# A graph layer in three-word float32 products: two samples as plain float32 products from raw weights, token rows moved to products 7 and 15, loads and buffers planned anew

## The chip, the cores and the metric

The kernel runs on one core of one Trainium2 chip. The metric is the device time of one execution in microseconds. The parts of the core have short names here, those of the profile: PE is TensorE (PEld its weight loads), DVE is VectorE, ACT is ScalarE, POOL is GpSimd, and SP is the queue from which nearly all DMAs are issued.

## The reference

There are 64 samples of 256 tokens with 768 features, and a 256x256 matrix of links for each. The links are 0 or 1 in the inputs of this case.

```python
h = relu(layernorm(x))                        # each [256, 768]
ctx = (adj @ (h @ Wadj.T + badj)) / max(deg, 1)
ctx += (adj.T @ (h @ Wrev.T + brev)) / max(rdeg, 1)
ctx += h @ Wself.T + bself
rel = agg @ Wr.T + br * deg                   # agg: sums over the links of E[rel]
rel += ragg @ Wrr.T + brr * rdeg
out = x + ctx + rel
```

With links of 0 and 1, everything in `rel` and all biases depend only on the two degrees of a token, so they come down to a product of a few "token rows" (degree and whether it is over zero) with a few rows made once from E, Wr, Wrr and the biases. What is left is three products of h with 768x768 weights, and two products with the links, called aggregates.

## The kernel before

**Fast products with 15 instead of 18.** A sample's h has two halves of 128 tokens (`a` and `b`), each cut in three along the features (`a0 a1 a2 b0 b1 b2`). The three weights are cut in three along the same dimension; block "21" is third 2 of weight 1 (0 is Wadj, 1 Wself, 2 Wrev). Together they are a matrix product of 2x3 by 3x3 blocks. The table `PRODUCTS` does it with 15 block products: each has a left side that is a sum of h blocks, and a right side that is a sum of weight blocks. Each block product is added to one or two of six results, `c00 c01 c02 c10 c11 c12` (token half, weight).

**Words.** [...]both sides are split in words: a left in three (`left0, left1, left2`), a right in three (`word0, word1, word2`), and a block product is three word products (L523, in `passes`). Each word product is 4 matmuls of 128x384 (two feature blocks, two halves of the outputs). Between them ACT multiplies the accumulator by a scale factor (`scale`, L559), and at the end ACT or DVE moves or adds it to its result (`read`, L568, L577, L579). Left words are made by ACT and DVE from h and from sums of h that POOL makes (L485 to L512). Right words are made once for each product in `prepare`: DVE sums raw weight blocks (`right`, L434), ACT and DVE take the words (L446 to L460). Products in `ON_PE` (11 and 3) have their sums and words formed on PE by plain float32 products with the identity (L397, L402), in a PSUM bank pair called `hold`.

**Two sweeps.** The words of 15 products don't fit beside the rest, so all 64 samples go through products 5, 10, 8, 11, 14, 3, 13 and 2 first, then all of them through 9, 7, 6, 15, 12, 4 and 1. Between the sweeps h and five of the results are stored to DRAM (`keep`) and loaded again. In sweep 1 `front1` loads x and its transpose, takes mean and variance on DVE (`bn_stats`, L598), turns them into a row on PE (the turn, L609), sends this through DRAM to all partitions (`d`, `row`), and POOL and DVE make h from them (centre L628, norm L632). In sweep 2 `front2` loads h, results and links, and makes token rows from the degrees; `step2` ends with high and low words of four results (`hl`, L762 and L766), the aggregates (L778, L789) and the store of the output. The token rows are added in `product` as two matmuls (L547) each in products 4 (rows of the half `a`, with weight -1, read into both c01 and c11), 12 (all, -1) and 1 (all, +1).

**A planner sets the order.** `record` notes each step with its engine, a duration in us, a rank (the time at which it is wanted, moved by a table `OFFSETS` of one number for each kind of step), and what it reads and writes. `Plan.schedule` then plays the engines: each takes the step of lowest rank that is ready, and the order that comes out is the order of the program. Each engine runs its steps in that order. Steps marked `lock` keep DVE and POOL out of each other's way. Buffers come in classes, handed out in order of rank, a slot being free once the last step on its buffer has ended: 

```python
SLOTS = {"W": 24, "B": 17, "T": 5, "A": 3, "S": 8, "Q": 4, "U": 2}
```

W holds two thirds-of-a-weight rows (6 KB a partition): raw blocks, words, hl pairs. B holds one row of 768 or a left's words: x, h, lefts, results, right sums. A holds links and rows, S small things, T sums of h, Q pairs of PSUM banks (one of them is `hold` in sweep 1), U the two halves of `hold`: turns, and copies of left0 that DVE subtracts from (`top`). The 8 products of sweep 1 have 24 words, as many as W has slots.

Of the kernel before, what the change touches and what calls it, by code (L numbers as in the profile page):

```python
# [14 lines left out]
ALU = mybir.AluOpType  # L15
# [39 lines left out]
    (  # L55
        (5, "y", 0, ((1, 1, 0),)),
        (10, "z", 0, ((1, 1, 2),)),
# [5 lines left out]
        (2, "z", 1, ((1, 0, 1),)),  # L63
# [3 lines left out]
        (7, "v", 0, ((1, 0, 1), (1, 0, 2))),  # L67
        (6, "x", 1, ((1, 0, 1),)),
        (15, "u", 0, ((1, 1, 1), (1, 1, 2))),
# [7 lines left out]
SLOTS = {"W": 24, "B": 17, "T": 5, "A": 3, "S": 8, "Q": 4, "U": 2}  # L77
ON_PE = (11, 3)
APART = ("22", "20", "00", "21", "01")
AHEAD = 5.0  # L80
OVERLAP = {"DVE": 0.08, "ACT": 0.095, "POOL": 0.045, "PE": 0.17}
PERIOD = (17.2, 21.4)
PREPARE = (6.0, 4.5)
LEAD = 5.0
OFFSETS = {
    "a0+a1+b0+b1": 6.92, "a0+a1+b0+b1@": 10.33, "a0+a2": -4.36, "a0+a2+b0+b2": -15.26, "a0+a2+b0+b2@": -101.36,
    "a0+a2+b2": -43.25, "a0+a2+b2@": 18.8, "a0+a2@": -65.24, "a1+a2": -1.7, "a1+a2@": -90.48, "a1+b0+b1": -2.76,
    "a1+b0+b1@": 37.03, "a1+b1": -4.89, "a1+b1@": 8.33, "a2+b2": -62.32, "a2+b2@": 0.73, "adj": 7.74,
    "adj@": 11.96, "agg00": -22.66, "agg00@": -1.8, "agg01": 14.01, "agg01@": -4.15, "agg10": 18.9,
    "agg10@": -19.08, "agg11": 18.57, "agg11@": -53.92, "aggr": -58.89, "aggr@": 7.86, "b0+b1": -35.52,  # L90
    "b0+b1@": 20.73, "b1+b2": -58.71, "b1+b2@": 9.34, "b2-a1": -78.11, "b2-a1@": 23.55, "bias": -93.82, "c00": 4.1,
    "c00@": -32.32, "c01": -13.38, "c01@": -25.73, "c02": -10.98, "c02@": -58.58, "c10": 15.35, "c10@": -16.49,
    "c11": 4.28, "c11@": 28.03, "c12": 5.06, "c12@": 22.74, "centre0": -2.99, "centre0@": 48.24, "centre1": -36.36,
    "centre1@": -19.74, "cols": 59.3, "d": 8.44, "d@": -26.79, "degree": 4.86, "degree@": -25.5,
    "diagonal": -16.03, "eT": -2.45, "eps": -58.84, "eps@": -14.98, "first 1": -13.18, "first 10": -32.05,
    "first 10@": 36.33, "first 11": -73.71, "first 11@": 12.34, "first 12": -23.58, "first 12@": 24.72,
    "first 13": 13, "first 13@": 11.63, "first 14": -45.99, "first 14@": -0.54, "first 15": -64.88,
    "first 15@": -7.01, "first 1@": -53.22, "first 2": -17.08, "first 2@": -7.79, "first 3": -22.76,
    "first 3@": 0.32, "first 4": -5.82, "first 4@": -10.53, "first 5": 2.67, "first 5@": -21.18, "first 6": 9.55,
    "first 6@": 9.11, "first 7": -39.56, "first 7@": -22.92, "first 8": 23.14, "first 8@": -81.1,  # L100
    "first 9": -31.59, "first 9@": 29.93, "flag": 58.21, "h0": -17.13, "h0@": -14.79, "h1": 5.1, "h1@": -12.91,
    "half": -17.88, "half@": 39.87, "high00": 15.93, "high00@": 11.46, "high02": 33.87, "high02@": -65.71,
    "high10": 25.4, "high10@": -16.28, "high12": 14.73, "high12@": 16.2, "keep c00": -2.76, "keep c00@": -66.74,
    "keep c01": -49.17, "keep c01@": -17.21, "keep c02": -13.78, "keep c02@": 16.72, "keep c10": 2.56,
    "keep c10@": 27.78, "keep c12": -24.16, "keep c12@": 54.25, "keep h0": 57.82, "keep h0@": -13.43,
    "keep h1": 50.58, "keep h1@": -14.32, "left0 1": -19.12, "left0 10": -0.78, "left0 10@": 2.36, "left0 11": 5.7,
    "left0 11@": -57, "left0 12": 8.66, "left0 12@": 24.55, "left0 13": -10.65, "left0 13@": -53.6,
    "left0 14": -7.4, "left0 14@": 10.04, "left0 15": 0.45, "left0 15@": 13.09, "left0 1@": 20.01,
    "left0 2": -12.83, "left0 2@": -17.63, "left0 3": -44.32, "left0 3@": -29.15, "left0 4": -4.81,
    "left0 4@": -12.38, "left0 5": -15.48, "left0 5@": -6.26, "left0 6": 2.81, "left0 6@": 24.35,  # L110
    "left0 7": -43.92, "left0 7@": 8.32, "left0 8": -31.57, "left0 8@": -6.64, "left0 9": -73.51,
    "left0 9@": -13.5, "left1 1": -49.91, "left1 10": -0.8, "left1 10@": 36.7, "left1 11": 0.1,
    "left1 11@": -17.36, "left1 12": -16.79, "left1 12@": 17.57, "left1 13": -27.91, "left1 13@": 14.45,
    "left1 14": 25.3, "left1 14@": -1.57, "left1 15": 15.44, "left1 15@": -42.21, "left1 1@": -89.54,
    "left1 2": -4.18, "left1 2@": -18.11, "left1 3": 12.77, "left1 3@": -67.25, "left1 4": 21.43,
    "left1 4@": -23.96, "left1 5": -21.51, "left1 5@": 43.61, "left1 6": -76.57, "left1 6@": -33.58,
    "left1 7": 12.56, "left1 7@": 3.34, "left1 8": -17.95, "left1 8@": -11.83, "left1 9": -33.48,
    "left1 9@": -40.82, "left2 1": 15.98, "left2 10": -45.72, "left2 10@": -5.31, "left2 11": 13.71,
    "left2 11@": 13.79, "left2 12": 17.14, "left2 12@": -36.12, "left2 13": -80, "left2 13@": -73.73,
    "left2 14": 27.23, "left2 14@": 27.84, "left2 15": 5.95, "left2 15@": -6.41, "left2 1@": -31.13,  # L120
    "left2 2": 15.55, "left2 2@": -37.29, "left2 3": -26.89, "left2 3@": 75.78, "left2 4": 28.79,
    "left2 4@": 23.04, "left2 5": -17.53, "left2 5@": -19.13, "left2 6": 4.2, "left2 6@": 31.92, "left2 7": -35.03,
    "left2 7@": 20.55, "left2 8": -3.06, "left2 8@": 34.27, "left2 9": 2.47, "left2 9@": -7.4, "less of": -8.17,
    "line": -16.84, "line@": -70.49, "load raw00": -11.53, "load raw01": -9.83, "load raw02": -2.61,
    "load raw10": -14.49, "load raw11": 0.43, "load raw12": -8.47, "load raw20": -2.81, "load raw21": -1.61,
    "load raw22": -10.89, "low00": -25.5, "low00@": 22.91, "low02": 6.14, "low02@": 45.31, "low10": -11.25,
    "low10@": -20.56, "low12": 27.22, "low12@": -26.51, "minus": -23.89, "minus@": -6.49, "norm0": 12.4,
    "norm0@": 48.54, "norm1": 5.92, "norm1@": 4.71, "out0": -45.84, "out0@": 42.05, "out1": 4.37, "out1@": 69.47,
    "pick": -1.48, "plus": -23.43, "plus@": -44.43, "pow": -36.89, "pow@": -93.72, "rd": -32.96, "rd@": -55.47,
    "read 1": -39.73, "read 10": -30.69, "read 10@": 2.04, "read 11": -26.47, "read 11@": 28.3, "read 12": 6.94,  # L130
    "read 12@": 27.17, "read 13": 3.76, "read 13@": 6.54, "read 14": 16.39, "read 14@": 26.9, "read 15": 25.66,
# [37 lines left out]
def kind_of(name):  # L169
    kind, _, last = name.rpartition(" ")  # L170
    if not last.isdigit():
        return name
    return kind + "@" if last == "0" and not kind.endswith(" of") else kind
# [915 lines left out]
```

## Time and profile before

| | us |
|---|---|
| median of 3 runs | 2620.19 (2619.38 to 2621.8) |
| the profiled execution | 2618.8 |
| its span | 2617.0 |
| PE busy | 2526.7 (97%) |
| PE weight loads busy | 2446.6 (93%) |
| DVE busy | 2209.1 (84%) |
| ACT busy | 1877.9 (72%) |
| POOL busy | 1312.8 (50%) |
| DMA, mean | 228 GB/s |

The span is what the profiler records, from the first instruction to the last; the execution's own time is 1.8 us more. Busy times of PE are modelled and overlap from one matmul to the next, so that a long row of matmuls always reads as fully busy; how fast PE advances is better read from the starts of its instructions in the timeline. The table of busy time by stretch, the chain of waits (followed back from the end, at each step to what released it) and the timeline are views of the same trace. A name such as "L523 PE MATMUL y<-word,left" is a line of the kernel, an engine, and output and inputs by the program's names.

### The profile page before, as it was taken

The page shows a single profiled execution, that of the slowest core. Times are in us where ns is not written, and L with a number is a line of the kernel's source. Part 1 is how long each engine was busy: PE and PEld are TensorE (multiplying, and loading weights), DVE is VectorE, ACT ScalarE, POOL GpSimd, SP SyncE. Part 2 cuts the span into 40 slices and gives each one's busy share as a digit, 9 for nine tenths or more (in the row PEclk, how much of TensorE's full clock was granted, in tenths as well). Part 3 has the DMA queues.
Part 4 walks back from the last instruction along what each step waited for, and adds up shares of the span by engine and source line. Part 5 has one row for each costly group of instructions (what it writes and reads, how often), then busy time and mean ns, then how long its engine had stood idle before and what let it go on. Part 6 is the DMA issues. An engine that isn't in the chain of part 4 may idle for free.

```text
span 2617.0 us, 44548 instructions
## 1 busy us (share of the span) xinstructions
PE 2526.7 (97%) x14154; PEld 2446.6 (93%) x14154; DVE 2209.1 (84%) x4007; ACT 1877.9 (72%) x4045; POOL 1312.8 (50%) x1160
## 2 busy tenths in 40 slices
PE   5999999999999999997999999999999999999998
PEld 2899999999999999986899999999999999999998
DVE  6877777777777777777999999999999999999997
ACT  4888888888888888887666666666666666666664
POOL 2454554445445445442555555555555555555554
PEclk8999999999999999998999999999999999999999
DMA  5677777777777777776566656555666666666563
GB/s 195 223 258 258 265 255 269 264 261 259 258 261 254 259 263 258 259 252 221 177 219 207 210 206 212 206 206 206 211 215 212 212 213 215 216 207 210 206 211 130
DMA packets 225815, 595.39 MB, mean 228 GB/s; under 512 B 24340, under 2 KB 24596, under 8 KB 225576
## 3 DMA queue, kind: packets, MB, share of 16 engines
q1 hardware_dynamic: 225576, 592.51, 65.1%
q8 instruction: 112, 1.84, 0.3%
q14 instruction: 127, 1.04, 0.1%
HBM read 365.79 MB, written 226.62 MB: 226 GB/s over the span
## 4 chain that ended last, share of the span: by engine, by line
PE 79%; DVE 6%; DMA 4%; ACT 4%; POOL 4%; issue 3%; SPq 0%; POOLq 0%; DVEq 0%; ACTq 0%
PE x L523 20%; PE y L523 13%; PE agg L778 13%; PE z L523 7%; PE w L523 6%; PE u L523 5%; PE v L523 5%; PE t L523 5%; DMA h<-in_x_t_dram 3%; POOL h L628 2%; PE x L547 2%; ACT hold L502 1%; ACT left L495 1%; DVE stats L598 1%; PE t L547 1%
## 5 line engine op out<-in xcount | busy, mean ns | idle before, releaser
L766 POOL TENSOR_TENSOR hl<-c,hl 128x768 fp32r<-128x768 f32 x256 | 506.3, 1978 | 628.4 <-DVE c L577 481.5
L523 PE MATMUL y<-word,left 128*128 128x384 f32 x3072 | 614.1, 341 | 14.1 <-ACT y L559 8.7
L523 PE MATMUL x<-word,left 128*128 128x384 f32 x3072 | 594.1, 337 | 3.2 <-DVE c L579 2.5
L523 PEld LDWEIGHTS y<-word,left 128*128 128x128 f32 x3072 | 529.9, 189 | 46.9 <-ACT y L559 19.1
L523 PEld LDWEIGHTS x<-word,left 128*128 128x128 f32 x3072 | 536.5, 188 | 7.0 <-DVE c L579 2.8
L778 PE MATMUL agg<-hl,a 128*128 128x384 f32 x2048 | 385.7, 334 | 0.4 <-POOL hl L766 0.4
L778 PEld LDWEIGHTS agg<-hl,a 128*128 128x128 f32 x2048 | 357.7, 188 | 0.8 <-POOL hl L766 0.8
L628 POOL TENSOR_TENSOR h<-h,row 128x768 f32<-128x768 f32 x128 | 236.9, 1851 | 159.5 <-DMA h<-in_x_t_dram 127.2
L523 PE MATMUL w<-word,left 128*128 128x384 f32 x1536 | 311.2, 337 | 2.3 <-ACT c L568 1.6
L523 PE MATMUL z<-word,left 128*128 128x384 f32 x1536 | 310.2, 336 | 2.5 <-DVE left L512 1.4
L762 ACT ACTIVATE hl<-c 128x768 fp32r<-128x768 f32 x256 | 208.3, 837 | 129.5 <-PE agg L778 122.3
L789 DVE SCALAR_TENSOR_TENSOR c<-agg,rd,c 128x768 f32<-128x768 f32 x256 | 260.0, 1017 | 24.1 <-PE agg L778 23.4
L523 PEld LDWEIGHTS w<-word,left 128*128 128x128 f32 x1536 | 270.3, 189 | 5.9 <-ACT c L568 2.4
L523 PEld LDWEIGHTS z<-word,left 128*128 128x128 f32 x1536 | 271.8, 188 | 4.2 <-ACT z L559 1.9
L559 ACT ACTIVATE x<-x 128x768 f32<-128x768 f32 x256 | 203.3, 795 | 71.0 <-PE x L523 37.3
L559 ACT ACTIVATE y<-y 128x768 f32<-128x768 f32 x256 | 199.7, 780 | 38.8 <-PE y L523 38.8
L632 DVE SCALAR_TENSOR_TENSOR h<-h,row 128x768 f32<-128x768 f32 x128 | 123.0, 961 | 114.5 <-POOL h L628 114.5
L512 DVE SCALAR_TENSOR_TENSOR left<-left,hold 128x256 fp32r<-128x256 f32 x512 | 203.5, 419 | 12.7 <-PE hold L397 3.3
L502 ACT ACTIVATE hold<-left 128x256 f32<-128x256 f32 x512 | 198.6, 388 | 21.2 <-DVE left L512 7.6
L512 DVE SCALAR_TENSOR_TENSOR left<-left 128x256 fp32r<-128x256 f32 x448 | 205.4, 482 | 2.1
L725 ACT ACTIVATE a<-adj 128x256 fp32r<-128x256 int32 x256 | 103.9, 408 | 87.8 <-PE agg L778 85.9
L523 PE MATMUL u<-word,left 128*128 128x384 f32 x768 | 155.8, 337 | 8.8 <-DVE left L508 6.7
(132 smaller groups left out, 4411.4 us busy)
## 6 DMA issues: line engine op xcount, KB each, us to landing
c<-kept SPq DMA_DIRECT2D x320, 384.0 KB
kept<-c SPq DMA_DIRECT2D x256, 384.0 KB
h<-in_x_t_dram SPq DMA_DIRECT2D x128, 384.0 KB
x<-in_x_dram SPq DMA_DIRECT2D x128, 384.0 KB
kept_h<-h SPq DMA_DIRECT2D x128, 384.0 KB
h<-kept_h SPq DMA_DIRECT2D x128, 384.0 KB
out_dram<-c SPq DMA_DIRECT2D x128, 384.0 KB
adj<-in_adj_dram SPq DMA_DIRECT2D x64, 512.0 KB
```

Source lines behind the costliest of these rows:

```text
L502: lambda: nc.scalar.activation(view(top), t(w)[:, 0].bitcast(F32), AF.Copy),
L512: lambda: nc.vector.scalar_tensor_tensor(t(w)[:, 2], t(w)[:, 1].bitcast(F32), -STEP, first(), op0=ALU.mult, op1=ALU.add), s == 1,
L523: nc.tensor.matmul(t(q)[:, half, : H // 2], t(w)[:, lw, f, :], t(r[rw])[:, f, ts(half, H // 2)], start=start and i == 0 and f == 0, stop=s ...
L547: nc.tensor.matmul(t(q)[:, half, : H // 2], t(rows[2])[rows[0]], v["rows"].tile[rows[0], ts(half, H // 2)], start=False, stop=False, skip_ ...
L559: lambda: nc.scalar.activation(view(), view(), AF.Copy, scale=scale),
L628: lambda h=h, one=one: nc.gpsimd.tensor_tensor(t(h), t(h), one(0), op=ALU.subtract),
L632: lambda h=h, one=one: nc.vector.scalar_tensor_tensor(t(h), t(h), 0.0, one(1), op0=ALU.max, op1=ALU.mult), True,
L725: lambda c=c, k=k: nc.scalar.activation(t(a)[:, c, k, :], t(adj)[:, c, k, :], AF.Copy, accum_out=t(deg)[:, b, c, 1 - k : 2 - k]),
L762: lambda: nc.scalar.activation(t(pair)[:, 0], t(o), AF.Copy, scale=LOWER),
L766: lambda: nc.gpsimd.tensor_tensor(t(pair)[:, 1], t(o), t(pair)[:, 0].bitcast(F32), op=ALU.subtract),
L778: nc.tensor.matmul(t(q)[:, half, : H // 2], t(s["a"])[:, c, k, ts(ic, P)], t(pairs[c])[:, part, ts(half, H // 2)], start=(c == 0 and part ...
L789: lambda q=q, to=to, ic=ic: nc.vector.scalar_tensor_tensor(to(), t(q)[:, :, : H // 2], t(rd)[:, ic, k : k + 1], to(), op0=ALU.mult, op1=AL ...
```

## The change

- Samples 0 and 63 leave the two sweeps. `whole` multiplies their h with the raw weights in plain float32, 72 matmuls of 128x384 for a sample: the three weights in three thirds for each token half. Sample 0 does so at the start, while the words of sweep 1 are formed, and its six results are stored. Sample 63 does so between the sweeps, while the words of sweep 2 are formed, and its results stay on the chip. The token rows of these two are products of their own, and their aggregates come right after the changeover. The sweeps have the 62 samples in between.
- The token rows go into products 7 and 15 after the first of the two results that these are read into: product 7 then gives c02 without and c01 with the rows, product 15 c12 and c11. Two matmuls in each, with the rows of one token half; those of products 4, 12 and 1 go, and so do `plus` and `minus`.
- Word 11 is formed on ACT and DVE instead of PE. Only product 14 has its raw block loaded apart. Words are prepared in the orders `OPENING` and `CHANGE`, at distances of 6.0 us instead of 6.0 and 4.5.
- Loads held back: `Plan.schedule` lets no engine but PE take a step whose rank is more than `PACE` (5 us) beyond that of PE's next step, and PE is asked first. The landing times of DMAs in the plan are 2.2 us for loads and 1.5 for stores instead of 2.0, and the row is counted as 400 KB instead of 256.
- Buffers shared anew: B has 18 slots instead of 17 and S 6 instead of 8; x1 of the 62 samples goes to class A; the rows made from E and the biases move from a tile of their own to a slot of B.
- In sweep 1 product 10 stands first and 2 third. `OFFSETS` has new values throughout, and values of their own for samples 0, 1, 62 and 63 (`MARK`).

The core of the diff; the line numbers of the changed kernel differ (`passes` is at L620, the rows at L644, `whole` at L762):

```diff
-SLOTS = {"W": 24, "B": 17, "T": 5, "A": 3, "S": 8, "Q": 4, "U": 2}
-ON_PE = (11, 3)
-APART = ("22", "20", "00", "21", "01")
+OPENING = (5, 8, 13, 11, 3, 10, 2, 14)
+CHANGE = (7, 15, 9, 12, 6, 4, 1)
+WHOLE = ((0, 2, 1), (2, 1, 0))
+SLOTS = {"W": 24, "B": 18, "T": 5, "A": 3, "S": 6, "Q": 4, "U": 2}
+ON_PE = (3,)
+APART = (14,)
+PACE = 5.0
...
+                    if e != "PE" and steps and o.rank > steps[-1].rank + PACE:
+                        passed.append(item)
+                        break
...
         for i, (sign, c, m) in enumerate(reads):
             key = (b, c, m)
+            if rows and i:
+                pe(2 * on_pe(H // 2) + 0.17, rank + 2.7, f"rows {n} {b}", [rows, v["rows"], q], [q], add_rows)
...
-        xs = [plan.buf("B", [P, H], F32, f"x{c}_{b}") for c in range(C)]
+        xs = [plan.buf("BA"[c and b in regular], [P, H], F32, f"x{c}_{b}") for c in range(C)]
...
+    def whole(b, s, rank):
+        for i, (m, c) in enumerate((m, c) for m in WHOLE[s] for c in range(C)):
+            at = rank + 7.8 * i
+            q = plan.buf("Q", [P, 2, 512], F32, f"whole{c}{m}_{b}")
...
+            for k in range(3):
+                r = load_raw(f"{k}{m}", s, at - 12.0, False)
+
+                def run(q=q, k=k, c=c, r=r):
+                    for f in range(2):
+                        for half in range(2):
+                            nc.tensor.matmul(
+                                t(q)[:, half, : H // 2], t(hT[b][c])[:, 2 * k + f, :], r[f][1]()[:, ts(half, H // 2)],
+                                start=k == 0 and f == 0, stop=k == 2 and f == 1,
+                            )
...
-        where = {
-            4: (slice(0, P), "half", s["half"]),
-            12: (slice(0, P), "minus", s["minus"]),
-            1: (slice(0, P), "plus", s["plus"]),
-        }
+        where = {7: s["half"][0], 15: s["half"][1]}
...
+    if part is None:
+        front1(0)
+        whole(0, 0, start1[0])
+        for i, n in enumerate(OPENING):
+            prepare(n, 0, 20.0 + gap1 * i)
+    for b in regular if part != 2 else ():
         front1(b)
         step1(b)
     if part is None:
+        front1(B - 1)
+        whole(B - 1, 1, last)
+        rows_prepare(last + 20.0)
+        for i, n in enumerate(CHANGE):
+            prepare(n, 1, last + 4.0 + gap2 * i)
...
+    order2 = [0, B - 1, *regular] if part is None else regular
```

## The prediction

> **What bounds the kernel now.** I read the page's busy line first (PE 97%), then cut the span at six landmarks of the PE timeline: the first product of sample 1, of sample 3 and of sample 63 in sweep 1 (85.63, 121.78, 1186.85), product 9 of sample 2 and of sample 63 in sweep 2 (1272.27, 2571.35). Columns: stretch, its length, busy time with count of PE, PEld, DVE, ACT, POOL, then TensorE clock, DMA share, GB/s.
>
> ```profile
> 0.00:85.63 85.63, 48.90 (x139) 30.20 (x140) 63.72 (x102) 41.47 (x75) 23.61 (x23) 0.86 0.52 184
> 85.63:121.78 36.15, 35.34 (x199) 33.80 (x199) 28.05 (x60) 30.68 (x63) 17.70 (x20) 1.00 0.74 255
> 121.78:1186.85 1065.07, 1044.43 (x5829) 996.14 (x5828) 810.19 (x1743) 885.44 (x1749) 519.20 (x541) 1.00 0.75 260
> 1186.85:1272.27 85.42, 61.08 (x274) 52.78 (x273) 74.07 (x110) 57.81 (x109) 28.54 (x18) 0.84 0.54 190
> 1272.27:2571.35 1299.08, 1299.08 (x7505) 1296.98 (x7505) 1200.71 (x1951) 844.16 (x2015) 706.31 (x552) 1.00 0.61 210
> 2571.35:2617.00 45.65, 37.91 (x216) 36.75 (x215) 32.39 (x45) 18.32 (x38) 17.46 (x10) 0.97 0.27 96
> ```
>
> Sweep 2 never leaves PE idle: 1299.08/61 = 21.30 us a sample for 122 matmuls of 384 columns and one turn. With 0.1 for a turn (my choice), a word matmul costs **0.1736 us**. Sweep 1 takes 1065.07/60 = 17.75 for 96 such matmuls (16.67) and a turn: about 1 us of each sample is stall. The chain of waits (start, us, what) shows where:
>
> ```profile
> 405.68 1.40 PE w L523 x8
> 407.08 0.02 issue
> 407.11 0.43 ACT left L495
> 407.54 0.02 issue
> 407.56 0.40 ACT hold L502
> 407.96 0.14 issue
> 408.09 0.30 PE hold L609
> 408.39 0.71 PE y L523 x4
> ```
>
> PE ends a product, ACT makes a left word only then, copies it into the hold bank, and the turn (L609) follows: 1.0 us without products. In the instruction order that left word waits for PE, as for a buffer of class B that the product still held. Now and then POOL waits for the sample's load as well:
>
> ```profile
> POOL h L628 <- DMA h<-in_x_t_dram: 127.2, 56, 5.5
> ```
>
> Price of a plain float32 matmul, from the timeline of L397 (24 matmuls, 48 records, so two records each):
>
> ```profile
> 20.23 2.76 PE L397 MATMUL hold<-raw,ident 128*128 128x384 f32 x4
> 22.79 0.96 PE L397 MATMUL hold<-raw,diagonal-1.0_0_641 128*128 128x384 f32 x2
> ...
> 58.98 1.45 PE L397 MATMUL hold<-raw,diagonal-1.0_0_641 128*128 128x384 f32 x4
> 60.27 0.81 PE L397 MATMUL hold<-raw,ident 128*128 128x384 f32 x2
> ```
>
> (22.79-20.23)/2 = 1.28 us early on, (60.27-58.98)/2 = **0.645 us** later.
>
> **What the Trainium skill says.** "TensorE: Matmul & The Clock Gate", part 1: the array runs at half clock until it was busy for about 3.4 us. The trace agrees: 1.28 against 0.645, and clocks of 0.86 and 0.84 only where PE has gaps. "FP8 and Floating Point Precision", TensorE Precision Notes: true fp32 takes four passes. Here 0.645/0.1736 = 3.7. "GPSIMD Engine Reference", section 1: POOL shares its SBUF interfaces with a DVE that has two SBUF inputs. Agrees: one hl subtraction of POOL, 1.86 us in the median, took 13.30 us from 1235.98, while words were formed.
>
> **Part by part.** In each stretch I count PE's instructions in the order of the program and price them: that is the floor, and what the stretch has above it is idle time of PE. Before, the opening has 24 plain and 88 word matmuls and 3 turns (15.5+15.3+0.3 = 31.1), then come 196 word matmuls and 2 turns (34.2), 5768 and 59 (1007.2), 262 with the 4 plain ones of the token rows and 2 turns (48.3), 7442 and 61 (1298.0), 213 and 1 (37.1). Together 2455.9, so **161 us of the span are idle**: 54.5, 1.9, 57.9, 37.1, 1.1 and 8.5. For after I count the changed program's order in the same way. Its landmarks are the first products of samples 1, 3 and 62 in sweep 1, and product 9 of samples 3 and 62 in sweep 2.
>
> *Samples 0 and 63 as whole float32 products.* Each loses 15x12 word matmuls (31.2 us) and gains 72 plain ones (46.4): 30 us more PE work for both. Their left words, scale steps and most of their keeps and reloads go too; they lay beside PE's work. Word 11 leaves PE for ACT and DVE: 12 plain and 8 word matmuls, -9.1; DVE gets eight full-row steps for four half ones, counted below.
>
> *Token rows* in 7 and 15: 4 matmuls instead of 6, in 62 samples: -21.5. 30.4-9.1-21.5 is nothing: **2455 of PE work** after as before. A gain must come out of the idle time.
>
> *Opening.* ACT makes line before any word, and only two raw loads lie ahead of the row. Before, d went out at 9.94, row at 12.99, and POOL got it at 19.83, behind three more raw loads. I take row at 15, centre 2.07, norm 0.95: whole products start at 18 (16 to 22). Then 84 plain and 8 word matmuls and 3 turns, 55.9, plus 1.7 for 3.4 us at half clock and 5.4 for word 3, which alternates PE, ACT and DVE on two hold slots (before, two such words cost PE some 12 us of waits for L411, L416 and L421). Sample 1 begins at **81** (77 to 89). DVE must be through by then: 46 full-row steps of 0.95 us (16 sums, 14 rests, 12 last words, 4 norms) plus 7.5 of small ones, 51 from about 10, plus about 8 for POOL's centres and raws landing, then 5 for the chain POOL, ACT, DVE to the first left: 75 to 80. So no slack, hence the upper end. Samples 1 to 3: 31.4 plus 3.6: **35** (33.5 to 38).
>
> *Sweep 1, 59 periods* to sample 62: 5668 matmuls and 59 turns, 989.9. Buffers: x1 moves to class A and B has 18 slots for 17, so two more. In the new order h loads go out a sample earlier, both centres lie together, and the left word of 10 waits for POOL only; those of 8 and 14 still wait for PE, but stand up to 36 and 76 matmuls (6 and 13 us) ahead of their use. The turn stands behind ACT's scale and left copy, a stall of 0.1 to 0.4. I take 0.3 a sample, 18: **1008** (6 to 48 of idle; the floor excludes less than nothing).
>
> *Changeover.* 368 word matmuls, 76 plain, 4 turns: 113.3. All 24 W slots hold words, so new raws load only as sample 62 ends products 10, 5, 11; 14 us of matmuls lie between the first freed slot and the first whole product, against a load of some 5. What is late next: raws and words. 38 word steps of 0.95 on DVE (four each for 7, 15, 9 and 12, six for 6, eight each for 4 and 1: 36; ACT's 28 of 0.84 are 24), sample 62 (13.5), 8 aggregate reads (8.2), other reads 8, one sample of sweep 2 (19.7): 85, under 113. Idle 8 (3 to 24): **121**.
>
> *Sweep 2, 59 periods.* 120 matmuls and a turn, 20.93; idle 4 in all (1 to 20): **1239**. The rows step waits for the first read of v or u on DVE; in the order 12 matmuls (2.1 us) lie between for 7, 24 (4.2 us) for 15; a read is 0.95. DVE has 19.7 of 20.93, so 1.2 us of it is free. ACT loses one 0.27 copy.
>
> *Tail.* 29.4 plus the same 8.5: **38** (36 to 41).
>
> S slots, offsets, PACE and landing times cost nothing of themselves: they only order the work, and what that does lies in the idle above. SP's queue issues 18 DMAs fewer (1566 rows for 1584); one raw block is loaded twice, 0.8 MB, in the opening, behind the row. DMA's share is 0.75 in sweep 1 and does not rise.
>
> Sum: 81+35+1008+121+1239+38 = **2522** of span, 67 of it idle. The execution profiled took 2618.8 for 2617.0 of span, and the median is 1.4 above it: +3, **2525 us**.
>
> **Rivals.** *A. Sweep 1 keeps its stall.* For: left 8 and 14 still wait for PE, the turn still for ACT. Against: two slots more. 57.9 for 18: 2565. *B. Slower: rows stall sweep 2.* If DVE comes to the first read a period's worth of queue late, PE stands at both rows steps, behind it all its later products. For: DVE 94% full, POOL shares its ports. Against: 12 and 24 matmuls in between. At 1 us each: 59x2 = +118, 2643; from 0.8 us each on it is slower. *C. The plain matmuls do not warm up* (PE in gaps behind DMA or words): 144x0.645 = +93, 2618, no change. For: PE ran at half clock until 48 us before. Against: each group is 2.6 us of solid work. That the change does not what it says is excluded by the instruction counts (13761 matmuls for 14125).
>
> **How the numbers follow.** Forecast 0.74, A 0.15, C 0.04, B 0.07. About 0.2% is what a measurement of this kernel can tell from no change. Faster 0.90, same 0.03, slower 0.07. All low ends give 2498, all high ones 2600; they will not fall together, so 2504 to 2584, which holds A.
>
> **What would show it.** Right: PE's first whole product near 18, records of 0.32 us from about 22; sample 1 near 81; 17.1 us a sample in sweep 1 with no load wait at POOL; changeover near 121 with clock 1.0; 20.9 to 21.0 in sweep 2. Wrong: a period over 17.5 or over 21.3, or a clock below 0.9 between 25 and 80 us.

## The result: 3.3% slower, and all of the loss in sweep 2

The changed kernel takes 2704.15 us in the median (2702.75 to 2707.07, 4 runs), the kernel before 2619.78 (2612.1 to 2621.8, 4 runs): a ratio of **1.0329**, with an interval of 1.0306 to 1.0352. The forecast was 2525. The profiled execution took 2703.03 for a span of 2701.3.

I cut the span at the landmarks that the prediction had set: the first products of samples 1, 3 and 62 in sweep 1 (78.54, 114.43, 1139.84), product 9 of samples 3 and 62 in sweep 2 (1256.73, 2662.17). Busy time by stretch, kernel after: stretch, its length, busy time with count of PE, PEld, DVE, ACT, POOL, then TensorE clock, DMA share, GB/s.

```profile
0.00:78.54 78.54, 58.71 (x179) 34.21 (x180) 55.01 (x82) 33.81 (x54) 19.22 (x18) 1.00 0.57 205
78.54:114.43 35.89, 34.57 (x185) 31.11 (x184) 30.01 (x65) 29.09 (x60) 19.57 (x20) 1.00 0.71 242
114.43:1139.84 1025.41, 1023.82 (x5729) 989.40 (x5729) 802.64 (x1707) 861.95 (x1709) 510.18 (x531) 1.00 0.77 265
1139.84:1256.73 116.89, 115.61 (x525) 93.16 (x525) 101.60 (x156) 79.12 (x161) 46.34 (x34) 1.00 0.67 226
1256.73:2662.17 1405.44, 1296.89 (x7140) 1276.05 (x7140) 1284.56 (x1885) 828.95 (x1891) 677.73 (x531) 0.98 0.57 189
2662.17:2701.30 39.13, 31.54 (x172) 29.15 (x171) 27.75 (x42) 14.42 (x29) 11.23 (x8) 0.96 0.19 68
```

| stretch | forecast | measured |
|---|---|---|
| to sample 1 | 81 | 78.5 |
| samples 1 and 2 | 35 | 35.9 |
| sweep 1, 59 periods | 1008 | 1025.4 (17.38 a sample) |
| changeover | 121 | 116.9 |
| sweep 2, 59 periods | 1239 | **1405.4** (23.82 a sample) |
| tail | 38 | 39.1 |

Five of six stretches lie within 4% of the forecast. The fifth row of the view holds the loss: 1405.44 us with PE busy for 1296.89, where the kernel before had PE busy without a gap, and DVE busy for 91% of the time. The clock there is 0.98, where all stretches ahead of it show 1.00. Against the kernel before: all up to sample 3 is 7.4 us shorter (114.43 for 121.78), sweep 1 with the changeover 8.2 shorter, sweep 2 with the tail 99.8 longer. That is the 84.3 us between the two spans. The stretch of sweep 2 has 59 periods here and 61 in the kernel before, so each sample costs more than this sum shows: 23.82 us for 21.30.

The waits of all engines in the kernel after, over the whole span (engine, line, waited for: us in total, times, longest):

```profile
POOL hl L902 <- ACT hl L898: 768.3, 130, 17.4
...
PE x L620 <- DVE c L925: 108.5, 57, 2.4
...
DVE c L674 <- PE v L644: 57.2, 60, 1.0
```

L620 is a product's matmul, L925 is DVE's read of an aggregate. The second line is the only wait of PE for another engine in the steady part of sweep 2: once in each sample it stands for 1.9 us, always at the first matmul of product 9. It never stands at the rows step (L644). There the wait runs the other way, in the third line: DVE waits for PE, once a sample.

Product 9 has no data from that read. What it needs is a PSUM pair: class Q has four, and the pair that product 9 takes is the one that aggregate 00, of the sample two before, held until DVE read it. The chain of waits (start, us, what) shows what DVE did until then:

```profile
2012.56 0.36 PE v L644 x2
...
2012.95 0.95 DVE c L674
...
2014.47 0.94 DVE c L676
2015.42 0.86 DVE c L674
...
2016.61 0.93 DVE c L925
...
2018.47 2.08 DVE left L609
2020.54 1.97 DVE left L605
2022.52 0.94 DVE c L925
...
2023.50 1.67 PE x L620 x8
```

This is a **ring**. PE takes 12.67 us from product 9 (2023.50) to the end of product 7's rows step (2036.17). DVE's second read of product 7 waits for that step, and behind it, in DVE's fixed order, stand two other reads, an aggregate read, seven left steps and last the read of aggregate 00 (L925 at 2022.52): 10.5 us. This frees the pair, and product 9 of the next sample starts. 12.67 and 10.5 make 23.2, and so long is the undisturbed round (product 9 at 1426.07 and at 1449.31: 23.24). PE's own work in a round is 21.2 us (the period of e6 below, in which PE does not wait), so PE stands for the rest.

Two steps of the ring are far too long. DVE's timeline of the same place (start, us, engine, line, operation, out and in, count):

```profile
2018.13 2.41 DVE L609 SCALAR_TENSOR_TENSOR left<-left 128x256 fp32r<-128x256 f32 x2
2020.46 2.05 DVE L605 TENSOR_TENSOR left<-a1+a,left 128x256 fp32r<-128x256 f32 x1
```

and POOL's:

```profile
2018.11 4.12 POOL L902 TENSOR_TENSOR hl<-c,hl 128x768 fp32r<-128x768 f32 x2 [2.96 <-ACT hl L898]
```

In the same timeline a left step alone is 0.41 us (at 2017.80), and two in a row are 0.75 (at 2025.64). Beside POOL's two subtractions of low words the pair takes 2.41 and the next step 2.05: 3.3 us more than alone. "SBUF — State Buffer", section "Who interferes with whom", of the Trainium skill says that a DVE instruction with two SBUF inputs and a GpSimd instruction that reads SBUF contend for a shared read interface, that this is an exclusive lock, and that the order of issue decides who is held up. The trace agrees. POOL's two subtractions, one by one:

```profile
2018.11 2.14 POOL L902 TENSOR_TENSOR hl<-c,hl 128x768 fp32r<-128x768 f32 x1 [2.96 <-ACT hl L898]
2020.22 2.01 POOL L902 TENSOR_TENSOR hl<-c,hl 128x768 fp32r<-128x768 f32 x1
```

The first of the two left steps passes in 0.41 us. The second (2018.47 in the chain) ends at 2020.55, 0.3 us after POOL's first subtraction, and the step of `a1+a` ends at 2022.51, 0.3 us after POOL's second one. POOL loses as well: its pair takes 4.12 here and 3.66 where no left step lies beside it (at 2009.91). The plan keeps such steps of POOL and DVE apart by its lock, but in the program only the order on each engine and the data are left of this. POOL waits for ACT's high word alone (the 768.3 us above), and starts when it comes.

DVE's groups from 1300 to 2500 us (busy us, mean ns of one, idle before), kernel after:

```profile
L609 DVE SCALAR_TENSOR_TENSOR left<-left 128x256 fp32r<-128x256 f32 x354 | 242.6, 708 | 1.7
L605 DVE TENSOR_TENSOR left<-a1+a,left 128x256 fp32r<-128x256 f32 x51 | 89.5, 1755 | 0.0
```

and of the kernel before, where L512 and L508 are the same two steps:

```profile
L512 DVE SCALAR_TENSOR_TENSOR left<-left 128x256 fp32r<-128x256 f32 x394 | 179.3, 479 | 1.9
L508 DVE TENSOR_TENSOR left<-a1+a,left 128x256 fp32r<-128x256 f32 x56 | 23.6, 422 | 0.0
```

What all left steps of a sample take over 0.415 us each (seven of the first kind and seven of the others) is the **stretch**: 1.8 us a sample before, 3.6 after. DVE's work was not the same in the new order.

An undisturbed round takes 23.24, but the mean period is 23.8, and the difference is the clock. The mean is made up of 21.2 of work, 1.9 of wait, 0.3 until the matmuls flow again (the eight of 2023.50 take 1.67 for 1.40), and some 0.3 a round because in 17 of 55 rounds the eight matmuls after the wait took more than 2.2 us; this adds up to 23.7. The last section comes back to it.

### The profile page after: what moved, and what is told of

It reads as the page before. It is cut to its first block, busy times and chain, and to the rows that moved or that the text cites. A ratio compares the mean times of both kernels' runs of the same rounds, so it can differ in the third digit from the quotient of the medians.

```text
span 2701.3 us, 43298 instructions
## 1 busy us (share of the span) xinstructions
PE 2561.1 (95%) x13922; PEld 2453.1 (91%) x13922; DVE 2301.6 (85%) x3933; ACT 1847.3 (68%) x3901; POOL 1284.3 (48%) x1138
## 4 chain that ended last, share of the span: by engine, by line
PE 35%; DVE 20%; issue 2%; ACT 0%; DVEq 0%; DMA 0%; POOL 0%; ACTq 0%; POOLq 0%
PE x L620 13%; PE agg L914 7%; DVE left L609 5%; DVE left L605 5%; PE v L620 5%; DVE c L925 4%; DVE c L674 4%; PE u L620 3%; PE t L620 2%; DVE c L676 2%; PE whole L762 2%; PE v L644 1%; PE y L620 0%; PE pt L883 0%; PE w L620 0%
## 5 line engine op out<-in xcount | busy, mean ns | idle before, releaser
L902 POOL TENSOR_TENSOR hl<-c,hl 128x768 fp32r<-128x768 f32 x256 | 494.0, 1949 | 775.5 <-ACT hl L898 768.3
L620 PE MATMUL x<-word,left 128*128 128x384 f32 x2976 | 623.9, 350 | 109.6 <-DVE c L925 108.5
L620 PEld LDWEIGHTS x<-word,left 128*128 128x128 f32 x2976 | 535.7, 193 | 131.3 <-DVE c L925 126.9
L620 PE MATMUL y<-word,left 128*128 128x384 f32 x2976 | 576.0, 338 | 1.1 <-ACT y L654 0.7
L620 PEld LDWEIGHTS y<-word,left 128*128 128x128 f32 x2976 | 525.5, 188 | 4.5 <-ACT y L654 2.5
L654 ACT ACTIVATE x<-x 128x768 f32<-128x768 f32 x248 | 197.2, 795 | 292.1 <-PE x L620 292.0
L914 PE MATMUL agg<-hl,a 128*128 128x384 f32 x2048 | 395.7, 340 | 0.0
L620 PE MATMUL w<-word,left 128*128 128x384 f32 x1488 | 313.9, 346 | 1.8 <-ACT c L665 1.3
L620 PE MATMUL z<-word,left 128*128 128x384 f32 x1488 | 307.4, 341 | 0.3 <-ACT z L654 0.2
L609 DVE SCALAR_TENSOR_TENSOR left<-left 128x256 fp32r<-128x256 f32 x434 | 291.0, 693 | 2.1
L620 PEld LDWEIGHTS w<-word,left 128*128 128x128 f32 x1488 | 256.1, 188 | 26.4 <-ACT w L654 24.5
L620 PEld LDWEIGHTS z<-word,left 128*128 128x128 f32 x1488 | 262.1, 189 | 2.0 <-ACT z L654 0.9
L925 DVE SCALAR_TENSOR_TENSOR c<-agg,rd,c 128x768 f32<-128x768 f32 x252 | 254.8, 1011 | 5.5 <-PE agg L914 2.8
L654 ACT ACTIVATE y<-y 128x768 f32<-128x768 f32 x248 | 197.6, 797 | 4.0 <-PE y L620 2.9
L609 DVE SCALAR_TENSOR_TENSOR left<-left,hold 128x256 fp32r<-128x256 f32 x496 | 194.9, 414 | 6.1 <-ACT hold L599 3.0
L674 DVE TENSOR_TENSOR c<-c,v 128x768 f32<-128x768 f32 x124 | 117.7, 949 | 57.4 <-PE v L644 57.2
L620 PE MATMUL t<-word,left 128*128 128x384 f32 x744 | 160.4, 353 | 0.1
L620 PE MATMUL v<-word,left 128*128 128x384 f32 x744 | 151.3, 338 | 0.1
```

The lines of the kernel that those rows point to most:

```text
L609: lambda: nc.vector.scalar_tensor_tensor(t(w)[:, 2], t(w)[:, 1].bitcast(F32), -STEP, first(), op0=ALU.mult, op1=ALU.add), s == 1,
L620: nc.tensor.matmul(t(q)[:, half, : H // 2], t(w)[:, lw, f, :], t(r[rw])[:, f, ts(half, H // 2)], start=start and i == 0 and f == 0, stop=s ...
L654: lambda: nc.scalar.activation(view(), view(), AF.Copy, scale=scale),
L674: emit = lambda to=to, op=op: nc.vector.tensor_tensor(to(), to(), view(), op=op)
L902: lambda: nc.gpsimd.tensor_tensor(t(pair)[:, 1], t(o), t(pair)[:, 0].bitcast(F32), op=ALU.subtract),
L914: nc.tensor.matmul(t(q)[:, half, : H // 2], t(s["a"])[:, c, k, ts(ic, P)], t(pairs[c])[:, part, ts(half, H // 2)], start=(c == 0 and part ...
```

## Experiments

The theory (T, where a text on record uses a letter): sweep 2 is held by the ring of product 9, rows step, DVE's queue, aggregate 00 and its PSUM pair, and the steps stretched by POOL make the ring longer than PE's work. The rivals: the rows steps are the cause (the prediction's rival B); DVE has simply too much work; the new table of ranks is bad as a whole, and no single place matters. All kernels but the last are edits of the kernel after. Two numbers tell them apart, both from the steady part of sweep 2: its period, and the stretch, worked out as above. The runs were made in four sittings, in which the kernel before took 2620, 2614, 2613 and 2619; each ratio is to the kernel before of the same sitting.

| kernel | median us | ratio to before | period | stretch |
|---|---|---|---|---|
| before | 2619.78 | | 21.30 | 1.8 |
| after | 2704.15 | 1.0329 (1.0306 to 1.0352) | 23.8 | 3.6 |
| e1, aggregate read one place earlier | 2616.72 | 1.0011 (1.0004 to 1.0018) | 22.35 | 2.8 |
| e2, low words on ACT | 2601.32 | 0.9953 (0.9936 to 0.997) | 22.10 | 1.4 |
| e3, no rows matmuls | 2735.86 | 1.0463 (1.0446 to 1.0481) | 24.42 | 4.1 |
| e4, rows back in 4, 12, 1 | 2625.2 | 1.0043 (1.0026 to 1.0059) | 22.37 | 1.6 |
| e5, eight places in the order | **2557.94** | 0.9789 (0.9773 to 0.9806) | 21.23 | 1.8 |
| e6, POOL's subtraction without its read | 2550.41 | 0.9758 (0.9742 to 0.9775) | 21.21 | 1.2 |
| e7, no PACE | 2712.42 | 1.0382 (1.0351 to 1.0412) | 22.19 | 1.4 |
| e8, e5's moves on DVE alone | 2653.97 | 1.0132 (1.0115 to 1.0149) | 22.97 | 4.0 |
| e9, e5's moves on POOL alone | 2666.87 | 1.0187 (1.0168 to 1.0205) | 23.17 | 3.5 |
| e10, the kernel before with POOL's pair closed up | 2670.38 | 1.0201 (1.0167 to 1.0235) | 22.16 | 3.2 |

### e1: the read of aggregate 00 one place earlier

A function on the finished order puts DVE's read `agg00` of sample b before `left1 7` of sample b+2. In the steady order it passes that one instruction.

```diff
+        if eng == "DVE" and name.startswith("agg00 "):
+            j = at.get(("DVE", f"left1 7 {int(name[6:]) + 2}"), i)
+            if at["PE", name] < j < i:
+                moves[i] = j
...
-        for o in plan.schedule():
+        for o in sooner(plan.schedule()):
```

> One DVE instruction moves one place: the read of the last aggregate of a sample (agg00) is issued ahead of the first step of product 7's left word, no longer behind it. Theory T (ring): in sweep 2 PE's product 9 waits for this read to free its PSUM slot, and the read stands on DVE behind the second read of v, which waits for PE's rows step of product 7. Ring of the changed kernel: 12.7 us on PE from product 9 to the rows step, 10.5 us on DVE from there to the end of the agg00 read, 23.2 us. The step that is passed took 2.0 us, so 21.2 us a sample instead of 23.8 (the half-clock matmuls after long waits go too): 2701 - 59*2.6 = 2548 us. Rival R1 (DVE is simply full: 21.8 us of work a sample and 2 us of unavoidable waits): an exchange of two instructions changes nothing, 2700. Rival R2 (the rows step itself stalls PE): 2700 as well.

One instruction's place gave back 87 us of 2704. That it fell short of the expected 2548 has its reason in PE's waits (the edit moves the lines by 14):

```profile
PE v L634 <- DVE c L688: 26.6, 41, 0.7
PE x L634 <- DVE c L939: 17.8, 12, 1.5
```

The old wait (the second line) came 12 times instead of 50. Product 7 now waits instead for DVE's earlier reads in the same round. The ring that was longest is broken, and the next one is 22.35 long.

### e2: low words on ACT

ACT makes the low words of the 62 samples as a scaled copy; the subtraction is left out. POOL no longer reads beside DVE.

```diff
+            if b in regular:
+                nc.scalar.activation(t(pair)[:, 1], t(o), AF.Copy, scale=LOWER)
+            else:
+                nc.gpsimd.tensor_tensor(t(pair)[:, 1], t(o), t(pair)[:, 0].bitcast(F32), op=ALU.subtract)
```

> The low words of the aggregates in samples 1 to 62 are written by ACT as a scaled copy and not by POOL as a subtraction (the subtraction is left out of the computation); nothing else moves. Theory T: of the 10.5 us on DVE in the ring some 3.4 us are stretch, because POOL's pair of subtractions (4.1 us) runs beside DVE's steps with two SBUF inputs. Without it the ring is 12.7 + 7.2 = 19.9 us, under PE's own 20.9, so sweep 2 runs at 20.9 to 21.2 us: 2530 to 2550 us. DVE busy falls from 21.8 to about 18.5 us a sample. R1' (DVE is full without the stretch, or the stretch has another cause): no more than 0.5 us a sample, over 2670. R2 (rows step alone): unchanged, 2700.

A miss: 22.10. The stretch went as expected, and `a1+a` is back at 416 ns. But ACT got four full rows more of work a sample, and came into the chain of waits itself:

```profile
2020.91 0.73 ACT hl L903
2021.67 0.80 ACT u L654
```

PE's second step of product 15 starts only after ACT's scale (L654), and this stands behind low words (L903). PE's largest wait in the list is for one of DVE's reads, ahead of product 7 (11.1 us in 51 waits from 1300 to 2500 us), as in e1. The edit took away one cost and put in another, so it says little on the ring; e6 was made for that.

### e3: no matmuls in the rows steps

The rows steps stay in the order and issue nothing, so the token rows are missing from the sums.

```diff
-                pe(2 * on_pe(H // 2) + 0.17, rank + 2.7, f"rows {n} {b}", [rows, v["rows"], q], [q], add_rows)
+                pe(2 * on_pe(H // 2) + 0.17, rank + 2.7, f"rows {n} {b}", [rows, v["rows"], q], [q], lambda: None)
```

> The rows steps of products 7 and 15 issue no matmuls in samples 1 to 62 (the token rows are left out of the computation); every other instruction keeps its place. Theory T: the wait of DVE at the second read of v (0.95 us a sample) goes, the stretch by POOL stays, so DVE with its 21.8 us a sample or the ring one read earlier sets the time: 21.8 to 22.5 us a sample, 2580 to 2625 us. Rival R2 (the rows step is the whole cause): PE's floor less 4 matmuls, 20.2 us a sample, about 2490. If the rows step is no part of it: 2690 or more.

A miss with the other sign: slower by 32 us than after, with four matmuls less in each sample. DVE no longer stands at the rows step, comes earlier to the left steps, and meets POOL's pair more fully: its group of left steps is at 784 ns (708 in after), and `a0+a` at 1465 where after had 411. The first of the two, of DVE's groups from 1300 to 2500 us:

```profile
L609 DVE SCALAR_TENSOR_TENSOR left<-left 128x256 fp32r<-128x256 f32 x344 | 261.8, 784 | 1.7
```

This takes the matmuls of the rows steps out as the cause: without them PE still waits at product 9, for 3.0 us instead of 1.9 (147.8 in 49 waits). An undisturbed round takes 23.8 here (product 9 at 1383.64 and at 1407.43); the rest of the 24.42 is again the clock.

### e4: the rows back in products 4, 12 and 1

The token rows are added as in the kernel before, six matmuls in three products, and the planner makes its order anew.

```diff
-        where = {7: s["half"][0], 15: s["half"][1]}
+        where = dict(zip((4, 12, 1), s["half"]))
```

> The changed kernel with the token rows back in products 4, 12 and 1 (6 matmuls, with the single-word group; the reads of 7 and 15 follow each other again), the planner's costs and offsets as changed. Rival R2 (moving the rows is what costs): 21.3 us a sample in sweep 2 as before, 2701 - 59*2.5 = 2553 us. Theory T: the second read of v no longer waits for a rows step, but what DVE has to do ahead of the agg00 read and what POOL does beside it are set by the new order of issue; between 21.3 and 23 us a sample, 2555 to 2650, and DVE's mean for the last left step tells which: near 0.42 us with a short period, 0.7 with a long one.

22.37 is inside the wide range of T and well above the 21.3 of the rival. The left steps (L609) are at 559 ns, between the two marks that were set. The order is another one in many places: PE waits for one of DVE's product reads now, 54 times for 0.6 us (31.2 in all). The run can't be put down to the rows alone.

### e5: eight places in the order of sweep 2

Nothing is added or taken away: five places on DVE and three on POOL are changed, for samples 3 to 59. Each line puts the first step, of the sample shifted by the number, directly ahead of the second. The aim was that the read of aggregate 00 comes earlier, and that POOL's pair of low words does not meet the left steps of the ring.

```diff
+STEADY = (
+    ("DVE", "agg00", -1, "left1 7", 1),
+    ("DVE", "left2 6", 0, "left1 4", 0),
+    ("DVE", "left2 9", 1, "left1 7", 1),
+    ("POOL", "a0+a2+b0+b2", 1, "low12", 0),
+    ("POOL", "a0+a2+b2", 1, "a0+a2+b0+b2", 1),
+    ("POOL", "low12", 0, "a0+a2+b0+b2", 1),
+    ("DVE", "left1 1", 1, "left1 12", 0),
+    ("DVE", "left1 6", 0, "read 9", 0),
+)
```

> The changed kernel with eight changes of order in sweep 2 (samples 4 to 60), no instruction added, removed or altered. On DVE the agg00 read and the second left word of product 9 come ahead of product 7's left steps, the left steps of product 6 go behind the agg11 read and the product 9 read, and one left step of product 1 is issued beside product 12's. On POOL the second low-word subtraction of a pair (low12) is put behind a short left sum, so that the pair no longer runs as one block of 4 us. Theory T (sweep 2 is set by a ring of waits through DVE, PE's PSUM slots and DVE again, which POOL's pair stretches; the amount of work is not the bound): with the steps ahead of the agg00 read and of the t reads moved away, both rings are shorter than PE's 20.9 us, and a sample takes 21.0 to 21.5 us: 2530 to 2565 us. Rival R1 (DVE has too much work for 21 us): DVE's busy time stays at 20.8 to 21.8 us a sample, the period stays at 22.1 us or more as in the two kernels with one change, 2600 or more. A third outcome, a new ring of another kind, would give 21.6 to 22.1: 2565 to 2600.

2557.94, faster than both kernels: 2.1% less than before, 5.4% less than after. Of PE's waits from 1300 to 2500 us 3 are left, where after had 50. DVE is busy for 19.9 us a sample with the same instructions, where after had 21.8, so it does not have too much work. Its group of left steps shows one part of the reason, a stretch down to that of the kernel before; e8 and e9 take the two parts apart.

```profile
L630 DVE SCALAR_TENSOR_TENSOR left<-left 128x256 fp32r<-128x256 f32 x394 | 231.2, 588 | 1.9
```

### e6: POOL writes and does not read

The low words are set to zero by a memset, so the subtraction is left out; the order stays that of after.

```diff
+            lambda: nc.gpsimd.memset(t(pair)[:, 1].bitcast(F32), 0.0) if b in regular else nc.gpsimd.tensor_tensor(
```

> In samples 1 to 62 POOL fills the low words of the aggregates with zeros and reads nothing for them (the subtraction is left out of the computation); ACT gets no work for it, unlike in the kernel in which ACT wrote them. Order of issue as in the changed kernel. Theory T: DVE's two-input left steps no longer stand behind POOL's pair, their mean falls from 0.70 to 0.42 us (L609) and from 1.78 to 0.42 (the first step of product 7), DVE's busy time from 21.8 to 18.5 us a sample; the ring is then 12.7 + 7.2 us, under PE's 20.9: 21.0 to 21.4 us a sample, 2530 to 2560 us. If the stretch is not POOL's two-input reading but something else (a write of POOL, DMA, the PSUM), it stays, and so does the time: 2680 or more. R1 (the order itself is too slow even without the stretch): 22 us a sample or more, 2600 or more.

The time is a hit: with the order of after untouched the period falls to 21.21, and PE has no wait at all from 1300 to 2500 us. DVE's group of left steps:

```profile
L609 DVE SCALAR_TENSOR_TENSOR left<-left 128x256 fp32r<-128x256 f32 x396 | 188.2, 499 | 1.9
```

The stretch does not go entirely: 0.42 us was expected for these steps, and 18.5 us a sample for DVE, which is busy for 19.7. Three things change at once, though. POOL does not read, its step is 0.74 us instead of 1.95, and it starts without the high word: POOL's wait is now for PE's aggregate and no longer for ACT. The ring keeps every other instruction. The same section of "SBUF — State Buffer" says that a GpSimd instruction that only writes doesn't contend with DVE's second input; the 499 ns (708 in after) agree with this. `a1+a` is at 952 (1755 in after).

### e7: no PACE

```diff
-PACE = 5.0
+PACE = 1e9
```

> The changed kernel with the planner's PACE taken away (the other engines' steps are no longer held back to 5 us of rank behind PE's next step); all else as changed, so that the whole order of issue comes out anew. If PACE made the tight order of sweep 2: nearer to the 21.3 us of before, some 21.9 us a sample, but sweep 1 a little slower, since loads and left words then take buffers early (17.5 us a sample for 17.4): about 2600 us in all. If the new offsets or the rows' place made it: 23 us or more in sweep 2, 2680 or more.

A miss. Sweep 2 falls to 22.19 with little stretch, but sweep 1 rises to about 18.9 a sample. And here rival B of the prediction takes place, PE standing at a rows step (PE's waits from 1300 to 2500 us):

```profile
PE u L644 <- DVE c L674: 30.7, 38, 1.9
```

At 0.8 us each, for one of the two rows steps. So that wait exists in other orders of the same steps, only not in that of after.

### e8 and e9: e5 by halves

e8 has e5's five lines for DVE, e9 the three for POOL.

> The five DVE moves of the reordered kernel without its three POOL moves. Theory T (order on DVE and POOL's block of two subtractions act together): the agg00 read and the t reads come earlier, but the left steps that stand behind them still meet POOL's block of 4 us; 21.7 to 23.0 us a sample, 2580 to 2655 us, and the mean of DVE's second left steps (L609's line) stays near 0.7 us. If the places of the two reads on DVE were all of it: 21.3, as with all eight moves, 2558. If POOL's block were all of it: 23.8, 2700.

> The three POOL moves of the reordered kernel without its five DVE moves: low12 no longer follows low02 directly, two short left sums come between the four subtractions in another place. Theory T: the left steps ahead of the agg00 read meet one subtraction in place of two; the first step of product 7 (1.78 us on average) falls to about 1 us, the ring of 23.2 us by 0.8 to 1.2: 22.0 to 23.1 us a sample, 2595 to 2660 us. If POOL's block were all of it: 21.3, 2558. If the places on DVE were all of it: 23.8, 2700.

e8 lies at the upper end of what was expected, e9 just above it. Neither half does it: they save 50 and 37 us where both save 146. PE's waits in e8 from 1300 to 2500 us (the edit moves the lines by 18):

```profile
PE x L638 <- DVE c L943: 76.9, 52, 1.5
```

In e8 POOL's pair still lands on the ring, only on another left step (`a0+a`, 1894 ns, where it was `a1+a`). In e9 PE waits at product 9 (52 times, 33.0 us) and at product 7 as well (52 times, 43.0 us). Moving what is stretched and moving what waits behind it are worth more together than their sum.

### e10: the kernel before with POOL's pair closed up

In the kernel before, POOL makes sums of h between two low words. This edit puts them next to each other, in samples 3 to 57, and changes nothing else.

```diff
+STEADY = (
+    ("POOL", "low00", -1, "a0+a2+b2", 0),
+)
```

> The kernel before with one exchange on POOL in sweep 2 (samples 3 to 57): the subtraction low00 is issued directly behind low10, ahead of three short left sums, so that POOL reads for nearly 4 us in one block as in the changed kernel; nothing else moves. Theory T: DVE's left steps that lie beside it are stretched by about 1 us more a sample, and the three sums and the left words that wait for them come 1.9 us later; DVE had 1.6 us of idle time a sample, so 0.5 to 1.3 us a sample come through to PE: 55 periods, 2640 to 2690 us, PE no longer without waits in sweep 2. If before's freedom from waits does not hang on where POOL's subtractions lie: 2613 to 2620, no change.

A hit. One place in POOL's order makes the kernel before 2% slower, with no PE instruction moved. The line, of DVE's groups from 1300 to 2500 us, of left steps that had 722 ns in the kernel before:

```profile
L522 DVE TENSOR_TENSOR left<-h,left 128x256 fp32r<-128x256 f32 x108 | 137.4, 1273 | 16.8 <-ACT left L509 16.8
```

Another group, `a0+a2+b`, fell from 1137 to 458 at the same time, so the stretch moved as well as grew. PE's waits for DVE (28 of them, 16.5 us) account for a part of the 0.86 us a sample only. The starts of PE's matmuls hold the rest: in the same 1200 us there are about 150 pauses of 0.1 to 0.3 us, 25 us in all, too short for the list of waits. What ends them I did not follow. The edit also makes the three sums come one subtraction later, and the run doesn't separate this from the stretch.

### What the runs settle

The stretch by itself doesn't give the period: e8 has more of it than after and is faster, e4 and e7 have less than before and are slower than it. What counts is whether it lies in the ring that is longest. That the ring holds sweep 2 of after is shown by e1, in which one read was moved. e6 and e9, in which only steps of POOL differ, show that POOL's pair lengthens it, and e10 that the same closeness, with the later sums that come with it, costs time in the kernel before too. The rivals fall: e3 is slower without the rows matmuls, e5 runs the same instructions at PE's own pace in another order, so the amount of DVE's work is not the cause, and e1 shows that a single place in the order matters. Open is which part of the change made the order so tight. The planner places everything anew for each of them, and e4 and e7, which take back one part each, give orders of their own. The old `OFFSETS` in the changed planner were not tried.

## Why the prediction was wrong

**Opening: right.** Whole products were to start at 18. The timeline of PE, kernel after:

```profile
18.50 14.99 PE L762 MATMUL whole<-raw,h 128*128 128x384 f32 x40 [10.48 <-DVE h L729]
...
58.08 13.07 PE L762 MATMUL whole<-raw,h 128*128 128x384 f32 x40
```

The first forty records take 14.99 us, a later forty 13.07, which is 0.33 each. In the first row of forty the starts lie 0.64 us apart until 21.86 and 0.32 from 22.35 on, as forecast, and the clock of the changeover is 1.00, so rival C falls. Sample 1 came at 78.54 for 81, the changeover at 116.9 for 121.

**Sweep 1: right in kind, two terms too small.** The floor of 989.9 leaves 35 us for the 18 of idle time that I took (6 to 48 allowed). Some 12 of the 35 are no idle time: inside a row of word matmuls one starts 0.1757 us after the other, where I had priced 0.1736. By the same count the kernel before has 0.174. It is about 0.176 in both sweeps of every edit of the changed kernel, and 0.174 in e10; no run shows why. The stall of the kernel before is gone: rival A's 58 did not come. A good part of the other 23 are small waits of the second steps of products 11 and 3 for ACT (waits from 114.43 to 1139.84):

```profile
PEld w L620 <- ACT w L654: 23.6, 114, 0.6
```

POOL's centre waits for the row now (49 times, up to 7.0 us) and no longer for the load of h, as foreseen, and PE does not wait for it.

**Sweep 2: the step that failed** is "Sweep 2, 59 periods. 120 matmuls and a turn, 20.93; idle 4 in all (1 to 20)". The floor was nearly right: e5 and e6 run at 21.2, which is 16 us more over 59 periods, the same dearer matmul. The idle term was not 4 but about 154 (1405.4 less 59 times 21.21). Two assumptions in it broke:

- "DVE has 19.7 of 20.93, so 1.2 us of it is free." The 19.7 were those of the order before, with 1.8 us of stretch in them. In the new order DVE is busy for 21.8 us a sample (1284.56/59), more than PE's work. I had cited POOL's and DVE's shared interface, with a subtraction of 13 us in the changeover beside it, and then took its share in sweep 2 as given, as if it belonged to the instructions and not to their order.
- I looked for new waits where the change adds one, at the rows steps, from PE's side. There PE had 2 to 4 us of matmuls in hand, and that held: PE never waits there. But DVE does, and of what stands behind it in DVE's queue I followed only the read itself. The aggregate read at the end of that queue frees a PSUM pair. In "they only order the work, and what that does lies in the idle above" the whole loss lay in a sentence that priced nothing.

**Rival B** had the sign and DVE as the engine that is late, and was given 7 in 100. Its place was wrong: not the rows steps, but the slot of product 9, and a price of 1.9 us and more once a sample instead of 1 us twice. The range ended at 2584, and even all high ends together gave only 2600, because sweep 2's upper bound of 20 was a guess at small stalls and no bound on a ring. Had the idle term held, the forecast would have been off by little: e5 measures 2558, and its 33 over 2525 are about the 17 of sweep 1 and the 16 of sweep 2's floor.

## What to carry to other kernels

With an engine over nine tenths busy and a fixed order, follow each wait that a change adds to the end of the waiting engine's queue: which buffers or PSUM pairs come free there, and who starts on them. If that leads back to the start, add the ring up and compare it with the period of the bounding engine. And treat the time of a two-input DVE step as a property of its neighbours on POOL: count in the new order, not in the old profile, which steps lie beside POOL's reads, since an exclusion that only a planner knows is not kept on the chip.

## What was not expected of the hardware

After short waits PE was sometimes slow. PE's timeline of the kernel after, product 9 of two samples one after the other:

```profile
1377.58 2.93 PE L620 MATMUL x<-word,left 128*128 128x384 f32 x8 [2.36 <-DVE c L925]
1402.27 1.67 PE L620 MATMUL x<-word,left 128*128 128x384 f32 x8 [1.75 <-DVE c L925]
```

Of 55 such groups in sweep 2 after waits of 1.7 to 2.4 us, 17 took more than 2.2 us instead of 1.67; of 57 in e3, after waits of about 3.0, 19 did; in e8, of 52 groups after waits of about 1.5 none was slow, of three after longer ones the one after 2.43 was. The typical slow one is 2.93, and the granted clock of the stretch is 0.98. "TensorE: Matmul & The Clock Gate", part 1, of the Trainium skill has the array fall back to half clock after an idle window of about 3.4 us, a window that runs freely. Here waits of half that length were enough in about a third of the cases.

The granted clock on record tells what picks the cases. In sweep 2 of the kernel after it is 0.5 in 20 spells of 3.41 us, and these begin whole multiples of 3.41 us apart. The wait before 1377.58 and the spell that follows it, in pieces of that length (columns as in the first view):

```profile
1373.88:1377.29 3.41, 1.35 (x8) 1.02 (x6) 3.41 (x3) 2.31 (x8) 3.05 (x3) 1.00 0.15 60
1377.29:1380.70 3.41, 3.12 (x10) 3.12 (x11) 3.06 (x6) 0.15 (x1) 0.80 (x2) 0.50 0.68 228
1380.70:1384.12 3.42, 3.42 (x21) 3.42 (x20) 2.72 (x5) 1.85 (x7) 0.00 (x0) 1.00 0.64 233
```

If the whole of sweep 2 is cut at such points, 24 of its 57 waits lie with 1.75 us or more in one piece, and 20 of these are followed by a spell in the next piece; none of the other 33 is. In e3 all waits with 1.94 us or more in one piece are followed by one, 19 in number, and none of the rest, which have up to 1.90. So it is the place of the wait on this grid, together with its length, that picks the cases. A round of 23.24 is 0.65 us short of seven pieces, and so the wait moves through the grid. The page's free-running window fits this; that a whole window must be idle does not. Why the border lies a little differently in the two kernels is open.
